# A four-layer network on one core: the scan layer's softplus sum moves to TensorE, and its gate product to GpSimd

## The chip, the core and the metric

The kernel runs on one core of a Trainium2 chip. The time is that of one execution on the device, in microseconds (us); three runs of the kernel before gave a median of 12193.51 us (12187.44 to 12204.01). The core's engines work side by side, each through its own queue in order, and wait for each other through semaphores: TensorE (PE; its weight loads are shown apart, as PEld), VectorE (DVE), ScalarE (ACT), GpSimd (POOL), and SyncE (SP), which here only issues DMA transfers. SBUF is the working memory of 128 partitions, PSUM the small memory that PE writes its results to; in this kernel PE, DVE and ACT work on PSUM, while all of POOL's operands lie in SBUF.

## The reference

Four layers run one after the other on 8 images of 64 channels and 64 x 64 pixels, all in f32. Only the first one is changed, a state-space layer that scans each image in four directions (N = 16 states, DI = 128 inner channels, L = 4096 positions):

```python
xz = einsum('bhwc,dc->bhwd', x, in_proj_w) + in_proj_b
xi, z = split(xz, 2, axis=-1)
xc = silu(dwconv3(transpose(xi), conv_w, conv_b))
...
dts = softplus(einsum('bkrl,kdr->bkdl', dts, dtproj_w) + dtproj_b)
def step(h, inp):
    u_t, dt_t, B_t, C_t = inp
    h = h * exp(dt_t[..., None] * A) + dt_t[..., None] * B_t[:, :, None, :] * u_t[..., None]
    return (h, einsum('bkcn,bkn->bkc', h, C_t))
...
y = ln(y, outnorm_g, outnorm_b, LN_EPS) * silu(z)
return einsum('bhwd,cd->bhwc', y, outproj_w) + outproj_b
```

The two places of the change are the sum inside `softplus`, which the kernel computes as relu(v) + ln(1 + exp(-|v|)), and the product with `silu(z)`, here called the gate. After this layer come an attention layer, an MLP with an inner training loop, and a second attention layer; nothing in them is touched.

## The kernel before

**Chunks and turns.** `scan_layer` goes through 8 images (b = 0 to 7). Each image has 16 chunks: four directions k times four stretches of CH = 1024 positions. Directions 0 and 1 run forward over rows and over columns, 2 and 3 backward; most images take them in the order 0, 2, 1, 3, so that chunk s = 0 to 3 of an image is direction 0, and so on. In a chunk there is one turn for each of the 16 states, n = 0 to 15. One turn works on tiles of 128 channels x 1024 positions:

- `decay` (L762, ACT): a = exp(dt * A), two turns ahead, into one of three buffers, each free again when DVE's scan of three turns before has read it.
- `spread` (L777 or L780), one turn ahead: brings the B row of state n into a PSUM tile `z` of two buffers. In four of the sixteen turns (`BY_POOL`, n = 0, 3, 6, 8) POOL has multiplied it by dt * u already (L770, three turns ahead, on a tile `bt` that DMA fetched), and ACT copies the product to PSUM. In the other twelve PE spreads it by two bf16 matmuls (L780). Buffer z(n) is free when the scan of turn n - 2 is done.
- `unit`: in those twelve turns DVE multiplies z by dt * u (L807); in all of them DVE runs the recurrence along the positions as one scan instruction (L811), and POOL multiplies the result h by the C row `ct` (L816).
- `sum_up` (L882): PE adds the products of all states into the PSUM tile `yps`, two f32 matmuls of 512 columns, LAG = 2 turns behind. In turn 3 it is left out, because `begin_sum` opens the tile of the new chunk there, and in turn 7 (`n == LAG + 5`) it is done twice to catch up.

DVE thus does per turn a scan and in three turns of four a multiply; a PE queue for turn n holds, in this order, `spread(n + 1)`, the sums, one background item, and what the hooks of the turn add.

**Background items.** All other work of the layer (projections of the next image, its layer norm and convolution, and the output of the image before) is cut into items, pairs `(make, use)`, that a `Background` queue hands out one per turn: `make` issues matmuls into a PSUM bank of the pool `psum` (two banks of 512 columns, tag `mm`), `use` takes the bank in the turn after, in `bg.after()`. What is handed to `bg.later` is issued at the start of the next `bg.after()`. In turns 6, 7, 8 (and 9, where the next chunk splits its B rows in three bf16 parts by `rest`, L730 to L736, which happens for directions 0 and 1) no item with matmuls is started. The first items of a chunk are those of `project` for the next chunk: `lower` (L630) and `step_size` (L650), whose result ACT turns into `dt` = relu(v) and `e` = |v| (L658, L659). A convolution (L534, nine taps) is spread over the rest of a chunk's turns in chunks 8 to 15 and holds one of the two banks all the while.

**The two places.** (1) `soft1`, `soft2` and `soft3` are hooked to turns 6, 7 and 8: e = exp(-e) and e = ln(1 + e) on ACT (L664, L667), dt = dt + e on POOL (L670). In turn 11 `step_input` makes dt * u on POOL (L689). The steps of the first four chunks of image 0 (early) and of the last two of image 7 (late) stand at other places. (2) `after`, an image's output, is queued in turn 4 of the next image's first chunk: the norm of y (`norm_y`), and then, for each of 8 blocks of 512 positions, `apply` (a DVE product L475 and an ACT pass L476), `gate` (PE makes z in PSUM, L578; ACT loads the table for Silu, applies it in place, L581, and loads the former table back by `exp_and_ln`, L340; DVE multiplies y by it, L589) and `project_out` (PE, L597 and L598; ACT to `xo`, L604; a DMA out). These items run in chunks 1 to 4 or so of an image, the next image's norm after them, then the convolutions.

Of the kernel before, what the change touches and what calls it, by code (L numbers as in the profile page):

```python
# [3 lines left out]

# [6 lines left out]
F32 = mybir.dt.float32  # L11
BF16 = mybir.dt.bfloat16
AF = mybir.ActivationFunctionType
ALU = mybir.AluOpType
# [230 lines left out]
def scan_layer(cm, x_in, w, xh):  # L245

    tc, nc = cm.tc, cm.nc
    with ExitStack() as ctx:
# [190 lines left out]
        def norm_y(y, blocks, load, gate, project_out):  # L439

            put, chain, sm = inverse_root(len(blocks))
            j0, nb, sq = blocks[0], len(blocks), {}

            def square(j):
                sq[j] = work.tile([128, BK], F32, name="sq", tag="sq")
                nc.scalar.activation(sq[j], y[:, bass.ts(j, BK)], AF.Square)

            def variance(j):
                def make():
                    ps = bank("vps1")  # L450
                    nc.tensor.matmul(
                        ps[:1], lno_avg[:, NBK - 1 : NBK], sq.pop(j), start=True, stop=True
                    )
                    return ps

                def use(ps):
                    put(ps, 1, j - j0)
                    if j + 2 in blocks:
                        square(j + 2)
                    if j - j0 < 3:  # L460
                        load(j)

                return make, use

            def apply(j):
                def make():
                    ps = bank("rps")

                    row = cm.ident[:nb, j - j0 : j - j0 + 1].to_broadcast([nb, DI])
                    nc.tensor.matmul(ps, row, sm["r"], start=True, stop=True)  # L470
                    return ps

                def use(ps):
                    v = y[:, bass.ts(j, BK)]
                    nc.vector.tensor_tensor(v, v, ps, ALU.mult)  # L475
                    nc.scalar.activation(v, v, AF.Identity, bias=on_b, scale=on_g)  # L476

                return make, use

            out = [(None, lambda _: [square(j) for j in blocks[:2]]), none]  # L480
            for j in blocks:
                out.append(variance(j))
            out += chain
            out += [apply(j) for j in blocks[:2]] + [gate(j0)]
            for j in blocks:
                if j + 2 in blocks:
                    out.append(apply(j + 2))
                out += [gate(j + 1) if j + 1 in blocks else none, project_out(j)]
            return out


        FIRST = (range(2), range(2, 3), range(3, 4))
# [71 lines left out]
        def after(b, y, block, blocks=range(NBK)):  # L564

            xf = x_in[b].rearrange("c h w -> c (h w)")
            gated = {}

            def load(j):
                xr = work.tile([C, BK], F32, name="xr", tag="xr", bufs=3)  # L570
                nc.sync.dma_start(xr, xf[:, bass.ts(j, BK)])
                gated[j] = xr

            def gate(j):
                def make():
                    ps = bank("zps")
                    half, x = block(j)
                    nc.tensor.matmul(ps, win[half, 1, :], x, start=True, stop=True)  # L578

                    def silu():  # L580
                        nc.scalar.activation(ps, ps, AF.Silu, bias=inb[:, 1:2])  # L581
                        exp_and_ln()

                    bg.later(silu)
                    return ps

                def use(ps):
                    v = y[:, bass.ts(j, BK)]
                    nc.vector.tensor_tensor(v, ps, v, ALU.mult)  # L589

                return make, use

            def project_out(j):
                def make():
                    po = bank("ops")
                    v = y[:, bass.ts(j, BK)]
                    nc.tensor.matmul(po[:C], cm.ident[:C, :C], gated[j], start=True, stop=False)  # L597
                    nc.tensor.matmul(po[:C], wout, v, start=False, stop=True)  # L598
                    return po

                def use(po):
                    del gated[j]
                    xo = work.tile([128, BK], F32, name="xo", tag="sq")
                    nc.scalar.activation(xo[:C], po[:C], AF.Identity, bias=outb)  # L604
                    bg.later(lambda: nc.sync.dma_start(xh[b][:, bass.ts(j, BK)], xo[:C]))
                    if j + 3 in blocks:
                        load(j + 3)

                return make, use

            return norm_y(y, blocks, load, gate, project_out)
# [8 lines left out]
        def project(u, k, c, low):  # L620

            uo = ordered(u, k, c)
            half = BK // S
            dt = work.tile([DI, CH], F32, name="dt", tag="dt")
            e = work.tile([DI, CH], F32, name="e", tag="e")

            def lower(i):
                def make():
                    ps = bank("dps")
                    nc.tensor.matmul(  # L630
                        ps[: 4 * N].rearrange("p (a b) -> p a b", b=S),
                        wx[:, k, :, :].rearrange("p a m -> p (a m)"),
                        uo[:, i * half : (i + 1) * half, :], start=True, stop=True,
                    )
                    return ps

                def use(ps):

                    nc.scalar.copy(e[: 4 * N, bass.ts(i, BK)], ps[: 4 * N])
                    bg.later(lambda: nc.sync.dma_start(  # L640
                        low["bc"].rearrange("a m l -> (a m) l")[:, bass.ts(i, BK)],
                        e[: 4 * N, bass.ts(i, BK)],
                    ))

                return make, use

            def step_size(i):
                def make():
                    ps = bank("tps2")
                    nc.tensor.matmul(  # L650
                        ps.rearrange("p (a b) -> p a b", b=S), wst[:, k, :],
                        uo[:, i * half : (i + 1) * half, :], start=True, stop=True,
                    )
                    return ps

                def use(ps):
                    b = dtb[:, k : k + 1]
                    nc.scalar.activation(dt[:, bass.ts(i, BK)], ps, AF.Relu, bias=b)  # L658
                    nc.scalar.activation(e[:, bass.ts(i, BK)], ps, AF.Abs, bias=b)  # L659

                return make, use

            def soft1(_=None):
                nc.scalar.activation(e, e, AF.Exp, scale=-1.0)  # L664

            def soft2(_=None):
                nc.scalar.activation(e, e, AF.Ln, bias=1.0)  # L667

            def soft3():
                nc.gpsimd.tensor_tensor(dt, dt, e, ALU.add)  # L670

            ut = {}

            items = [step_size(0), step_size(1)]
            if k < 2:
                low["bc"] = dr.tile([2, 2 * N, CH], F32, name="bc", tag="bc", bufs=8)
                items = [lower(0), lower(1)] + items
            if k % 2:
                ut["u"] = work.tile([DI, CH], F32, name="ut", tag="ut", bufs=1)
                uo = ut["u"].rearrange("p (a b) -> p a b", b=S)  # L680
                nc.scalar.copy(uo, ordered(u, k, c))
                items.insert(0, none)
            else:
                ut["u"] = u[:, bass.ts(c, CH)]
            return dt, ut, e, items, (soft1, soft2, soft3)
# [256 lines left out]
        with tc.manual_schedule():  # L942
# [16 lines left out]
            for b in range(NB):  # L959
                for s in range(4 * NCH):  # L960
# [11 lines left out]
                    if nxt:  # L972
                        do = nxt["pieces"]
                        if early:
                            hooks = {
                                12: [do[0]], 13: [nxt["soft"][2], lambda: step_input(nxt)] + do[1:5],
                                14: do[5:6], 15: do[6:],
                            }
                        else:
                            hooks = dict(zip((5, 7, 8, 9, 10, 13) if parts else (13,), ([f] for f in do)))  # L980
                            for i, f in zip((6, 7, 8), nxt["soft"]):
                                hooks[i] = hooks.get(i, []) + [f]
                            hooks[11] = hooks.get(11, []) + [lambda: step_input(nxt)]

# [6 lines left out]
                    for n in range(N):  # L991
# [6 lines left out]
                        else:  # L998
                            if len(pending) > LAG:
                                sum_up()  # L1000
                            if n == LAG + 5:
                                sum_up()
                            bg.before(n in idle, slots)
                        if (n + 5) % N in BY_POOL and not (early and n + 5 == N):
# [1189 lines left out]
```

## Time and profile before

| | |
|---|---|
| median of three runs | 12193.51 us (12187.44 to 12204.01) |
| profiled execution, own time | 12199.93 us |
| its span, first to last instruction | 12198.2 us |
| mean granted TensorE clock | 0.952 |
| first scan starts / last scan starts | 91.7 / 6916.1 us |
| `ct` products on POOL (L816) | 2048 x 2369 ns |
| `dt + e` on POOL (L670) | 128 x 2364 ns |
| scans on DVE (L811) | 1536 x 2341 ns and 512 x 2281 ns |
| multiplies on DVE (L807) | 1536 x 1211 ns |

Chunks 0 to 15 of image 3 begin at 2684.57, 2734.92, 2786.49, 2841.89, 2899.73, 2957.65, 3010.01, 3062.47, 3116.07, 3166.13, 3219.41, 3270.43, 3321.46, 3371.52, 3423.41 and 3476.83 us (the first scan of each); image 4 follows at 3527.9.

How to read the lines: a timeline line has the start, the duration, the engine, the source line, the operation with the tile written and those read, the shape, and how many instructions in a row it stands for; in brackets, how long the engine had been idle and what ended that. A matmul's duration contains its way through the array, so matmuls that follow each other closely overlap: the distance of two starts is what one costs. The same holds, by less, for DVE and POOL. A line by group has the busy time, the mean duration, and the idle time in front of the group. A line of the waits has the total, the number and the longest.

### The profile page before, as it was taken

To read this page: it belongs to the slowest core of one execution; us is meant where nothing else is said; L and a number is where in the kernel's file an instruction comes from. 1 tells how busy PE (TensorE), PEld (TensorE's weight loads), DVE (VectorE), ACT (ScalarE), POOL (GpSimd) and SP (SyncE) were. 2 spreads that over 40 slices of the span, in tenths; PEclk is the share of its full clock that TensorE was granted. 3 is DMA by queue.
4 is the path that set the end of the run, shared out by engine and by line. 5 is a ranking of instruction groups with operands and counts; after the bars stand their busy time and mean duration, and the time that the engine had idled before them with its cause. 6 is when DMAs were issued, how large, how long until landed. Compare 5 with 4: busy or idle time off the path is not lost. (4 is left out here: it accounts for less than half of the span.)

```text
span 12198.2 us, 120204 instructions
## 1 busy us (share of the span) xinstructions
PE 11171.0 (92%) x39087; PEld 4099.5 (34%) x39087; DVE 10381.2 (85%) x7400; ACT 7575.8 (62%) x10304; POOL 7249.5 (59%) x3326
## 2 busy tenths in 40 slices
PE   7899999999999999999998799999987779999999
PEld 2233333333333333333322233232335463333333
DVE  4999999999999999999999776868677686667767
ACT  4666667767667676676675554646547574555554
POOL 4999999999999999999999600000006490000000
PEclk8999999999999999999999899999998789999999
DMA  3666666666666666666666400000011100000000
GB/s 111 204 212 214 209 209 214 215 211 208 212 212 210 213 214 208 212 215 209 203 203 213 143 24 25 6 24 7 17 42 40 41 22 24 19 4 19 5 11 6
DMA packets 522900, 1528.64 MB, mean 125 GB/s; under 512 B 125312, under 2 KB 142352, under 8 KB 519696
## 3 DMA queue, kind: packets, MB, share of 16 engines
q1 hardware_dynamic: 522256, 1520.80, 37.9%
q8 instruction: 313, 5.13, 0.2%
q14 instruction: 331, 2.71, 0.1%
HBM read 1439.63 MB, written 72.09 MB: 124 GB/s over the span
## 5 line engine op out<-in xcount | busy, mean ns | idle before, releaser
L816 POOL TENSOR_TENSOR ct<-ct,h 128x1024 f32<-128x1024 f32 x2048 | 4796.4, 2369 | 297.0 <-DVE h L811 123.9
L882 PE MATMUL yps<-ct,lno_cen 128*128 128x512 f32 x8192 | 4119.2, 633 | 59.2 <-ACT yps L869 57.8
L811 DVE TENSOR_TENSOR_SCAN h<-a,state,z 128x1024 f32<-128x1024 f32 x1536 | 3571.0, 2341 | 84.0 <-ACT z L777 40.8
L762 ACT ACTIVATE a<-dt,amat 128x1024 f32<-128x1024 f32 x2048 | 2346.9, 1147 | 1136.5 <-DVE h L811 1132.3
L1191 DVE TENSOR_TENSOR sum<-sum,ex 128x1024 f32<-128x1024 f32 x1920 | 2347.9, 1223 | 633.0 <-ACT ex L1184 497.9
L1184 ACT ACTIVATE ex<-sc 128x1024 f32<-128x1024 f32 x2048 | 1968.1, 1024 | 1342.4 <-PE sc L1179 1342.0
L882 PEld LDWEIGHTS yps<-ct,lno_cen 128*128 128x128 f32 x8192 | 1475.9, 195 | 2077.1 <-issue 1810.5
L807 DVE TENSOR_TENSOR z<-z,e 128x1024 f32<-128x1024 f32 x1536 | 1860.0, 1211 | 125.2 <-PE z L780 77.7
L1198 PE MATMUL av<-ex,v 128*64 128x512 f32 x8192 | 1950.0, 604 | 0.0
L1179 PE MATMUL sc<-q,k 16*128 16x512 f32 (+1 forms) x8192 | 1562.2, 623 | 7.3 <-ACT q L1172 6.2
L780 PE MATMUL z<-bs,pick 48*128 48x512 bf16 x3072 | 940.6, 387 | 396.6 <-DVE h L811 348.4
L811 DVE TENSOR_TENSOR_SCAN h<-a,z 128x1024 f32<-128x1024 f32 x512 | 1162.0, 2281 | 81.3 <-ACT z L777 67.3
L770 POOL TENSOR_TENSOR bt<-bt,e 128x1024 f32<-128x1024 f32 x512 | 1212.9, 2369 | 5.2 <-PE cps L392 5.2
L1505 POOL TENSOR_TENSOR gt<-gt,pad 128x1024 f32<-128x1024 f32 x16 | 34.9, 2183 | 1574.3 <-ACT gt L1504 1574.3
L1198 PEld LDWEIGHTS av<-ex,v 128*64 128x64 f32 x8192 | 512.2, 136 | 1332.8 <-issue 1278.9
L1179 PEld LDWEIGHTS sc<-q,k 16*128 16x128 f32 (+1 forms) x8192 | 528.3, 184 | 1021.6 <-issue 976.6
L777 ACT COPY z<-bt 128x1024 f32<-128x1024 f32 x512 | 519.8, 1015 | 402.9 <-DVE h L811 302.9
L780 PEld LDWEIGHTS <-pick 48*128 48x128 bf16 x3072 | 175.4, 95 | 1515.4 <-DVE h L811 930.9
L534 PE MATMUL vps<-pad,convd 128*128 128x512 f32 x1152 | 574.8, 600 | 0.0
L1878 DVE RECIPROCAL r<-e 128x512 f32<-128x512 f32 x128 | 420.7, 3323 | 0.0
L1881 POOL TENSOR_TENSOR r<-r,half 128x512 f32<-128x512 f32 x128 | 162.7, 1271 | 366.7 <-issue 189.4
L798 ACT COPY state<-h 128x1 f32<-128x1 f32 x2048 | 363.1, 177 | 0.0
(417 smaller groups left out, 9581.1 us busy)
## 6 DMA issues: line engine op xcount, KB each, us to landing
ct<-bc SPq DMA_DIRECT2D x2048, 512.0 KB
bt<-bc SPq DMA_DIRECT2D x512, 512.0 KB
x<-x SPq DMA_DIRECT2D x12, 2048.0 KB
bc<-e SPq DMA_DIRECT2D x128, 128.0 KB
x<-x SPq DMA_DIRECT2D x32, 512.0 KB
part<-x SPq DMA_DIRECT2D x128, 128.0 KB
bsd<-bp SPq DMA_DIRECT2D x192, 64.0 KB
bs<-bsd SPq DMA_DIRECT2D x128, 96.0 KB
```

The source lines that it names most:

```text
L534: nc.tensor.matmul(held[0].rearrange("p (r c) -> p r c", c=S), convd[:, t, :], pad[:, j * rows + dy : (j + 1) * rows + dy, dx : dx + S], s ...
L762: ctl["exp", n] = nc.scalar.activation(ctl["a", n], ctl["dt"], AF.Exp, scale=amat[:, ctl["k"], n : n + 1])
L770: nc.gpsimd.tensor_tensor(bt, bt, ctl["dus"], ALU.mult)
L780: nc.tensor.matmul(z[:, bass.ts(i, BK)], pick[:, n : n + 1].to_broadcast([3 * N, DI]), ctl["bs"][:, bass.ts(i, BK)], start=True, stop=True,)
L807: first = nc.vector.tensor_tensor(z, z, ctl["dus"], ALU.mult)
L811: nc.vector.tensor_tensor_scan(h[:, flip], a[:, flip], z[:, flip], 0.0 if state is None else state[:, n : n + 1], ALU.mult, ALU.add,)
L816: freed[at] = nc.gpsimd.tensor_tensor(ct, ct, h, ALU.mult)
L882: nc.tensor.matmul(ctl["ps"][:, bass.ts(i, BK)], lno_cen, ct[:, bass.ts(i, BK)], start=False, stop=(n == N - 1 and not ctl["turns"]),)
L1179: nc.tensor.matmul(sc[:, e, :], k[r : r + d, bass.ts(j, 128)], qs[i][r : r + d, :], start=True, stop=True,)
L1184: nc.scalar.activation(ex, sc, AF.Exp)
L1191: nc.vector.tensor_tensor(sums[i], sums[i], ex, ALU.add)
L1198: nc.tensor.matmul(avs[i][r, :], v[:, j, r], ex[:, e, :], start=(j == 0), stop=(j == TQ - 1))
```

## The change

The softplus sum of a chunk (outside the early and late ones) is made by PE: for each half of 512 columns an identity matmul of `dt` and one of `e` into one PSUM bank, which ACT copies back to `dt` one turn later. The hooks move to turns 5 (exp), 6 (ln), 7 (first half) and 8 (second half), and the second `sum_up` from turn 7 to turn 6. In the gate, ACT's Silu goes from PSUM to a new SBUF tile `zg` one turn later than before (in `use` rather than by `later`), and POOL makes the product with y one turn after that; `project_out(j - 1)` rather than `project_out(j)` is queued behind `gate(j + 1)`. `zg` shares a tag of two buffers with `sq` and `xo`.

```diff
             for j in blocks:
                 if j + 2 in blocks:
                     out.append(apply(j + 2))
-                out += [gate(j + 1) if j + 1 in blocks else none, project_out(j)]
-            return out
+                if j + 1 in blocks:
+                    out.append(gate(j + 1))
+                elif nb < 3:
+                    out.append(none)
+                if j - 1 in blocks:
+                    out.append(project_out(j - 1))
+            return out + [project_out(blocks[-1])]
...
                     nc.tensor.matmul(ps, win[half, 1, :], x, start=True, stop=True)
-
-                    def silu():
-                        nc.scalar.activation(ps, ps, AF.Silu, bias=inb[:, 1:2])
-                        exp_and_ln()
-
-                    bg.later(silu)
                     return ps
 
                 def use(ps):
                     v = y[:, bass.ts(j, BK)]
-                    nc.vector.tensor_tensor(v, ps, v, ALU.mult)
+                    z = work.tile([DI, BK], F32, name="zg", tag="sq")
+                    nc.scalar.activation(z, ps, AF.Silu, bias=inb[:, 1:2])
+                    exp_and_ln()
+                    bg.later(lambda: nc.gpsimd.tensor_tensor(v, v, z, ALU.mult))
...
-            def soft3():
-                nc.gpsimd.tensor_tensor(dt, dt, e, ALU.add)
+            def soft3(i=None):
+
+                if i is None:
+                    nc.gpsimd.tensor_tensor(dt, dt, e, ALU.add)
+                    return
+                ps = bank("sps")
+                at = bass.ts(i, BK)
+                nc.tensor.matmul(ps, cm.ident, dt[:, at], start=True, stop=False)
+                nc.tensor.matmul(ps, cm.ident, e[:, at], start=False, stop=True)
+                bg.later(lambda: nc.scalar.copy(dt[:, at], ps))
...
-                            for i, f in zip((6, 7, 8), nxt["soft"]):
+                            soft = nxt["soft"]
+                            softs = soft if late else (soft[0], soft[1], partial(soft[2], 0), partial(soft[2], 1))
+                            for i, f in zip((6, 7, 8) if late else (5, 6, 7, 8), softs):
                                 hooks[i] = hooks.get(i, []) + [f]
...
-                            if n == LAG + 5:
+                            if n == LAG + 4:
                                 sum_up()
```

More of the change, by code (lines that the diff above doesn't have):

```diff
@@ L3 @@
 from contextlib import ExitStack
+from functools import partial
 import concourse.bass as bass
```

## The prediction

> **What bounds the kernel now.** I read the page's first two parts, then busy time by stretch, then the timelines of VectorE (DVE), GpSimd (POOL) and TensorE (PE) in single chunks, and the waits last. The change touches only the scan layer, the first 57% of the span, where three engines look full:
>
> ```profile
> PE 11171.0 (92%) x39087; PEld 4099.5 (34%) x39087; DVE 10381.2 (85%) x7400; ACT 7575.8 (62%) x10304; POOL 7249.5 (59%) x3326
> ```
> ```profile
> 400.00:6400.00 6000.00, 5647.02 (x13198) 1951.69 (x13196) 5839.45 (x3343) 4156.01 (x6164) 5811.44 (x2506) 0.97 0.64 211
> ...
> 3219.41:3270.43 51.02, 50.30 (x125) 18.14 (x123) 50.59 (x29) 35.95 (x55) 51.02 (x23) 1.00 0.71 222
> ```
>
> The columns are length, then PE, weight loads, DVE, ACT and POOL busy, clock, DMA. The last line is one chunk of sixteen turns (image 3, chunk 10). Which of the three decides is seen from starts, not from busy time:
>
> ```profile
> 3241.39 4.59 DVE L811 TENSOR_TENSOR_SCAN h<-a,state,z 128x1024 f32<-128x1024 f32 x2
> 3245.89 1.21 DVE L807 TENSOR_TENSOR z<-z,e 128x1024 f32<-128x1024 f32 x1
> 3247.14 2.35 DVE L811 TENSOR_TENSOR_SCAN h<-a,state,z 128x1024 f32<-128x1024 f32 x1
> 3249.40 1.21 DVE L807 TENSOR_TENSOR z<-z,e 128x1024 f32<-128x1024 f32 x1
> 3250.64 2.35 DVE L811 TENSOR_TENSOR_SCAN h<-a,state,z 128x1024 f32<-128x1024 f32 x1
> ```
>
> Scan to next start is 2.25 us, multiply to scan 1.24. Sixteen scans and twelve multiplies make 16 x 2.25 + 12 x 1.24 = 50.9 us: the whole chunk (51.02). DVE has no gap, so it is the bound. POOL's products follow each other at 2.32 us (four of L816 in 9.32 us), 22 in a chunk: 51.0. It is level with DVE, but what it makes early (bt) has turns to spare.
>
> PE must hand DVE a new `z` in 12 of 16 turns. Its timeline in turns 6 to 9 of the same chunk:
>
> ```profile
> 3238.54 0.60 PE L780 MATMUL z<-bs,pick 48*128 48x512 bf16 x2
> 3239.07 5.42 PE L882 MATMUL yps<-ct,lno_cen 128*128 128x512 f32 x12
> 3244.42 0.60 PE L780 MATMUL z<-bs,pick 48*128 48x512 bf16 x2
> 3244.95 1.98 PE L882 MATMUL yps<-ct,lno_cen 128*128 128x512 f32 x4
> 3246.77 0.59 PE L730 MATMUL brps<-bw,ident 128*128 128x256 f32 x2
> 3247.20 0.27 PE L732 MATMUL brps<-bp,minus 128*128 128x256 bf16 x1
> 3247.41 0.60 PE L780 MATMUL z<-bs,pick 48*128 48x512 bf16 x2
> ```
>
> No gap here either. An f32 matmul over 512 columns is two records; twelve records from 3239.07 to 3244.42 are 0.43 us each (less a small switch), so 0.86 us per instruction. z(7) starts at 3238.54, z(9) at 3244.42, z(10) at 3247.41. How late may z be? Where DVE does wait for it, the multiply starts 0.81 us after z's first matmul (chunk 13 of the same image):
>
> ```profile
> 3392.15 0.60 PE L780 MATMUL z<-bs,pick 48*128 48x512 bf16 x2
> ...
> 3398.03 0.60 PE L780 MATMUL z<-bs,pick 48*128 48x512 bf16 x2
> ```
> ```profile
> 3392.96 1.23 DVE L807 TENSOR_TENSOR z<-z,e 128x1024 f32<-128x1024 f32 x1 [0.62 <-PE z L780]
> ...
> 3398.84 1.23 DVE L807 TENSOR_TENSOR z<-z,e 128x1024 f32<-128x1024 f32 x1
> ```
>
> So chunk 13 has no slack at z(9); chunk 10 has 3245.89 - 3244.42 - 0.81 = 0.66 us. PE is the hidden second bound, just in these turns.
>
> **The change, part by part.** Counts come from the two programs' instruction orders: POOL -58, DVE -64, ACT +244, PE +488 matmuls, SP none.
>
> **(a) Softplus sum.** 122 of 128 adds `dt + e` leave POOL (2.32 us each, 283 us; the first chunk, three early and two late ones keep theirs). In their place PE gets four identity matmuls (4 x 0.86 = 3.44 us per chunk, 420 us in all) and ACT two copies from PSUM (about 0.58 us each by the 512-column copy L846).
>
> POOL's relief is worth nothing by itself where DVE has no gap: between 0 and the few gaps it causes (DVE's multiply waits 5.0 us on POOL in the stage). I take 0.
>
> The matmuls stand in turns 7 and 8, two in each, in PE's own order: z(7), three sums (the caught-up one moves from turn 7 to 6, still between z(7) and z(9): neutral), sum 0, z(9), one sum, (L730, L732), sum 1, z(10). So z(9) is 1.72 us later and z(10) 3.44. DVE then stalls by the delay less the slack, and after a stall its own clock has moved:
>
> - Chunk 10: z(9) late by 1.72 - 0.66 = 1.06. z(10) starts 3247.41, used 3249.40, slack 1.18: 3.44 - 1.18 - 1.06 = 1.20. Together 2.26.
> - Chunk 13: 1.72 - 0; z(10) starts 3400.48, used 3402.37, slack 1.08: 0.64. Together 2.36.
> - Chunk 5 (no convolution): z(9) 2983.95, used 2985.44, slack 0.68; z(10) 2986.40, used 2988.98, slack 1.77. Together 1.67.
> - Chunk 1: z(9) 2760.19, used 2761.68; z(10) 2763.18, used 2765.21. Together 2.22.
> - Chunk 3 (gates, DVE itself waiting): PE sits idle 1.57 us ahead of z(9), slack 1.29, then 2.34 at z(10). Together 0.
>
> Chunks 8 to 15 are like 10 and 13 (2.3), 0 to 2 like 1 (2.2), 4 to 7 like 5 (1.67), 3 is 0: (8 x 2.3 + 3 x 2.2 + 4 x 1.67) / 16 = 1.98 us, x 122 = **+242 us**. What PE still lags behind turn 10 (1.2 us) it makes up in the gaps of the next chunk's first turns (z(1) of chunk 13 waits 1.80 us for DVE), but where those are short (chunks 0, 8, 9) some stalls come again: between 0 and one more 1.2 us in three chunks of eight images (29), I take +15.
>
> The Trainium skill ("Perfetto Trace Analysis", Identifying the Most-Contended Engine) says matmul busy time tells little of PE's headroom and to judge by the busy share of weight loads. That share is 34%, which would leave room for all 488 matmuls and make this term 0. The twelve starts 0.43 us apart with no gap say otherwise for these turns, and I go by them.
>
> ACT: soft1 and soft2 move to turns 5 and 6, next to step_size's own two ACT passes. An ACT burst there can hold z(8)'s copy: in chunk 10 it has 1.2 us of slack against one pass of 1.05. 0 to +0.2 us per chunk, and a stall there would be taken out of the one at z(9): 0. Where a convolution holds one of the two PSUM banks and `brps` needs one too (chunks 8, 9, 10, 15), sum 1 waits for the cast of brps, 0.37 us and a handover, about 0.5: 0 to 32 x 0.5 = 16, I take +8.
>
> **(b) Gate.** 64 multiplies leave DVE:
>
> ```profile
> L589 DVE TENSOR_TENSOR y<-zps,y 128x512 f32<-128x512 f32 x48 | 32.2, 670 | 6.8 <-ACT zps L581 6.4
> ```
>
> Start to next start it is 0.58 us (2004.47 to 2005.05): 64 x 0.58 = **-37 us**, all on DVE's path. POOL gets 64 of about 1.27 us (128x512 products L1881), 81 us, less than the 283 it lost. The rule against it is in the Trainium skill ("GPSIMD Engine Reference", Engine selection): elementwise work belongs on VectorE, twice as fast. By the two durations alone that would cost 64 x 0.60 = +38; but DVE is the engine without a gap.
>
> Silu now runs one turn after its matmul rather than in the same turn, so ACT no longer stands waiting for PE:
>
> ```profile
> ACT zps L581 <- PE zps L578: 44.4, 30, 4.8
> ACT L581 <- PE zps L578: 42.6, 13, 6.8
> ```
>
> DVE's longest gaps of the stage (2.42 us before the scan of turn 6 in image 3, chunk 3, ended by ACT's copy of z) come from such bursts. That gap recurs in chunks 3 and 4 of an image, 8 x 2 x 2.2 = 35 at most. Table loads and Silu itself stay, ACT gains copies: 0 to -35, I take -15.
>
> New waits: Silu writes a buffer of two (shared with xo), so it waits for POOL's product of an earlier gate, and the last project_out waits for POOL where it waited for DVE. Behind Silu stand ACT's decays, which have two turns to spare. 0 to 8 x 1.5 = 12, I take +4. At the layer's end two gates lie in a bare chain: 2 x 0.6 = +1.
>
> Sum: 242 + 15 + 8 - 37 - 15 + 4 + 1 = **+218 us** on the profiled execution, 12199.9 (span 12198.2). The median of the three times, 12193.5, is 6.4 lower, so 12193.5 + 218 = **12412 us**, 1.8% slower.
>
> **Rivals.**
>
> 1. *Faster.* PE is not the bound in turns 7 to 9: the stall per chunk stays under 0.43 us, where 122 of them equal the gains of 37 + 15. For it: chunk 3 absorbs everything, and PE has over 2 us of gaps per chunk elsewhere. Against it: the four other chunks I read have 0 to 0.68 us of slack at z(9) against 1.72. With no stall the time is 12193 - 37 - 15 = 12141; if POOL's relief and ACT's also close half of the 165 us that DVE idles before its scans and multiplies (65.5 + 68.1 + 32.0 from 400 to 6900): 12193 - 52 - (83 - 15) = 12073.
> 2. *Slower by far less.* z(9) is absorbed and only z(10) stalls: between z(9) and z(10) PE needs a sum (1.82), sum 1 (1.72) and z (0.53) = 4.07, where DVE needs 3.5. That is 0.57 per chunk: 122 x 0.57 - 52 = +18, 12211.
> 3. *Slower by far more.* All 3.44 us add to every chunk (no slack counts, PE becomes the bound throughout): 420 - 37 = 12577.
> 4. *POOL's gate product becomes the wait.* If ACT waits for POOL one product (2.3 us) at each gate: 64 x 2.3 = +147 on top, 12559. For it: POOL at 5811 of 6000 us. Against: it loses 283.
>
> **How the numbers follow.** Forecast 0.74 (12290 to 12510); rival 1 0.09; rival 2 0.08; rivals 3 and 4 0.09. The low end cuts rival 1 and part of rival 2, the high end reaches half way to rivals 3 and 4: 12260 to 12530. About 0.2% (24 us) is what a measurement here tells from no change: rival 2 straddles it, half same, half slower. Faster 0.09, same 0.04, slower 0.87.
>
> **What the profile after would show.** Right: the DVE multiplies of turns 9 and 10 idle for 1 to 2 us each before them, ended by PE's z, in most chunks from 5 on; PE without gaps from turn 5 to 15; POOL's share down by 200 us and idle more; no DVE gate lines; chunks 8 to 15 near 53 us rather than 51. Wrong: those gaps absent and chunks still 51 us; or gaps ended by ACT's z copy (then the copies are to blame), or by POOL. What would make it wrong most: a turn-6 start of PE earlier than 1.3 us after DVE's scan of turn 5, as sums moved forward fall into gaps I counted as full.

## The result and the profile after

The changed kernel takes 12418.03 us (median of 4 runs, 12416.46 to 12424.47), the kernel before 12192.65 in the same series: a ratio of 1.0182 with a 95% interval of 1.0166 to 1.0198, 1.8% slower. The forecast was 12412 us.

The loss lies in the scan layer to the last microsecond: the last scan starts at 7135.2 us instead of 6916.1, 219.1 later, and the span is 218.5 longer. The first line is the page's busy time of the changed kernel; the second, its busy time in the same stretch as shown of before (length, PE, weight loads, DVE, ACT, POOL, clock, DMA).

```profile
PE 11506.0 (93%) x40063; PEld 4259.5 (34%) x40063; DVE 10364.8 (83%) x7336; ACT 7714.7 (62%) x10548; POOL 7061.7 (57%) x3268
```
```profile
400.00:6400.00 6000.00, 5765.36 (x13705) 2037.43 (x13704) 5649.84 (x3185) 4141.53 (x6194) 5454.93 (x2368) 0.99 0.62 204
```

In these 6000 us DVE is busy 5650 instead of 5839 and POOL 5455 instead of 5811: both stand idle more than before. Chunk 13 of image 3 shows why; this is PE's timeline, turns 6 to 9:

```profile
3487.87 0.60 PE L791 MATMUL z<-bs,pick 48*128 48x512 bf16 x2
3488.40 5.42 PE L893 MATMUL yps<-ct,lno_cen 128*128 128x512 f32 x12
3493.65 1.02 PE L679 MATMUL sps<-dt,ident 128*128 128x512 f32 x2
3494.51 1.02 PE L680 MATMUL sps<-e,ident 128*128 128x512 f32 x2
3495.47 0.60 PE L791 MATMUL z<-bs,pick 48*128 48x512 bf16 x2
3496.00 1.98 PE L893 MATMUL yps<-ct,lno_cen 128*128 128x512 f32 x4
3497.82 1.02 PE L679 MATMUL sps<-dt,ident 128*128 128x512 f32 x2
3498.68 1.02 PE L680 MATMUL sps<-e,ident 128*128 128x512 f32 x2
3499.63 0.60 PE L791 MATMUL z<-bs,pick 48*128 48x512 bf16 x2
```

From z(7) to z(9) PE needs 3495.47 - 3487.87 = 7.60 us; before the change it was 5.88. DVE's timeline of the same turns has the wait:

```profile
3489.94 4.59 DVE L822 TENSOR_TENSOR_SCAN h<-a,state,z 128x1024 f32<-128x1024 f32 x2
3496.28 1.23 DVE L818 TENSOR_TENSOR z<-z,e 128x1024 f32<-128x1024 f32 x1 [1.75 <-ACT dt L681]
3497.54 2.35 DVE L822 TENSOR_TENSOR_SCAN h<-a,state,z 128x1024 f32<-128x1024 f32 x1
3500.37 1.23 DVE L818 TENSOR_TENSOR z<-z,e 128x1024 f32<-128x1024 f32 x1 [0.48 <-ACT dt L681]
```

The prediction had 1.72 and 0.64 for this chunk. The multiply starts 0.81 us after z(9)'s first matmul, as it did before wherever DVE waited for PE. But the trace names something else as what ended the wait: ACT's copy of the sum to `dt`.

```profile
3495.57 0.59 ACT L681 COPY dt<-sps 128x512 f32<-128x512 f32 x1 [2.02 <-PE sps L680]
```

From 400 to 6900 us that name has the largest total of DVE's waits, which is why it needed an experiment:

```profile
DVE z L818 <- ACT dt L681: 190.4, 189, 2.2
...
DVE z L818 <- PE z L791: 49.9, 81, 2.2
```

All gaps of DVE over 0.06 us between the first and the last scan, added up from the trace, are 204 us before and 439 after; those ahead of turns 9 and 10 alone (of their multiply or scan) 38 and 239. The 235 us more of gaps, 22 us because an instruction behind a gap no longer starts before the one ahead of it has ended (in the lines of before, a scan of 2.35 us is followed after 2.25), and 37 us less of work on DVE make up the 219 us, to 1 us.

### The profile page after: what moved, and what is told of

It reads as the page before. It is cut to its first block, busy times and chain, and to the rows that moved or that the text cites. A ratio compares the mean times of both kernels' runs of the same rounds, so it can differ in the third digit from the quotient of the medians.

```text
span 12416.7 us, 122384 instructions
## 1 busy us (share of the span) xinstructions
PE 11506.0 (93%) x40063; PEld 4259.5 (34%) x40063; DVE 10364.8 (83%) x7336; ACT 7714.7 (62%) x10548; POOL 7061.7 (57%) x3268
## 5 line engine op out<-in xcount | busy, mean ns | idle before, releaser
L893 PE MATMUL yps<-ct,lno_cen 128*128 128x512 f32 x8192 | 4065.3, 626 | 59.0 <-ACT yps L880 58.8
```

The costliest lines, as they stand in the source:

```text
L893: nc.tensor.matmul(ctl["ps"][:, bass.ts(i, BK)], lno_cen, ct[:, bass.ts(i, BK)], start=False, stop=(n == N - 1 and not ctl["turns"]),)
```

## The experiments

**Each part alone.** *Gate only:* the kernel before with the new gate.

```diff
-                    bg.later(silu)
...
-                    nc.vector.tensor_tensor(v, ps, v, ALU.mult)
+                    z = work.tile([DI, BK], F32, name="zg", tag="sq")
+                    nc.scalar.activation(z, ps, AF.Silu, bias=inb[:, 1:2])
+                    exp_and_ln()
+                    bg.later(lambda: nc.gpsimd.tensor_tensor(v, v, z, ALU.mult))
```

> The kernel before with part (b) alone (gate product on GpSimd, Silu a turn later). Theory A (the loss is all in the identity matmuls of turns 7 and 8; the gate is a gain): 64 x 0.58 = 37 us of VectorE work go, and the gap before the scan of turn 6 in gate chunks (5.4 us per image in the kernel before, 0 in the changed one) goes too, 43 at most: 12193 - 37 - (15 to 43) = 12113 to 12141 us. Theory B (the gate product, queued on a GpSimd engine that is as full as VectorE, costs part of the loss): no gain or slower than 12193, since GpSimd's adds of the softplus sum are back here.

Measured: 12178.9 us against 12187.7, ratio 0.9994 (0.9984 to 1.0003). Not told from no change: the gain of theory A is not there. Theory B's "no gain" came true, but that a full POOL is the reason isn't shown by it (*room on GpSimd*, below, tests that). *Sum only:* the changed kernel with the gate of before.

```diff
-                    z = work.tile([DI, BK], F32, name="zg", tag="sq")
...
+                    nc.vector.tensor_tensor(v, ps, v, ALU.mult)
```

> The changed kernel with the gate as before: part (a) alone. Theory A: the changed kernel without the gate's gain, 12418 + 37 + (15 to 43) = 12470 to 12498 us, if the two parts add up. Theory B: below 12418.

Measured: 12454.9, ratio 1.0218 (1.0201 to 1.0235): not below 12418 as theory B had it, but 15 us short of theory A's range too, which took the two parts to add up. So the sum costs 267 us, and where it is in place the gate gives back 37 (12455 to 12418, which come from different series; 42 if each is taken against the kernel before of its own series); alone it gives 9. The two ratios of the 37 carry intervals of 0.0016 and 0.0017 to each side, some 28 us for the difference, so that the gate gave more beside the sum than alone is likely rather than shown.

**PE or ACT.** *Matmuls alone:* four identity matmuls in turns 7 and 8 of the kernel before, on constant data, read by nothing.

```diff
+            def load_pe():
+                ps = bank("sps")
+                m = convd[:, 0:4, :].rearrange("p a b -> p (a b)")
+                nc.tensor.matmul(ps, cm.ident, m, start=True, stop=False)
+                nc.tensor.matmul(ps, cm.ident, m, start=False, stop=True)
...
+                            if not late:
+                                for i in (7, 8):
+                                    hooks[i] = hooks.get(i, []) + [nxt["extra"]]
```

> The kernel before, GpSimd's add and hooks kept, with the four identity matmuls added in turns 7 and 8 on constant data into a bank that nothing reads (their result is not used). No ACT copies, no moved soft steps, gate as before. Theory A: the same stalls of z in turns 9 and 10, 242 + 15 + 8 = 265 us: about 12458 (12400 to 12500). Theory C: 12193, no change.

Measured: 12453.9, ratio 1.0218 (1.0201 to 1.0235): as expected by theory A, and the same as the whole of part (a), with some 29 us of uncertainty on the difference. With no copy there to be named, the trace now names PE. The first line is from the kernel before, the second from this run:

```profile
DVE z L807 <- PE z L780: 41.3, 46, 2.9
```
```profile
DVE z L815 <- PE z L788: 252.7, 264, 2.2
```

*Copies alone:* the other half (the edit is shown against *matmuls alone*).

```diff
-                nc.tensor.matmul(ps, cm.ident, m, start=True, stop=False)
-                nc.tensor.matmul(ps, cm.ident, m, start=False, stop=True)
+                bg.later(lambda: nc.scalar.copy(ps, convd[:, 0:4, :].rearrange("p a b -> p (a b)")))
```

> The kernel before with only the two ACT copies of 512 columns added, in turns 8 and 9, from a constant in SBUF into a PSUM bank that nothing reads (their result is not used). Theory A (TensorE alone): no loss, 12188 to 12200 us. Theory C (ACT's copies): up to the 230 us of the change.

Measured: 12182.0 against 12187.2, ratio 0.9997 (0.9988 to 1.0006). ACT's copies cost nothing (at most 7 us by the interval); theory C falls. These copies don't wait for PE as those of the changed kernel do (2.02 us in the line above); that the real ones cost nothing either follows, within the 29 us, from *sum only* being no slower than *matmuls alone*. In the changed kernel the copy of one half and z(9) both follow the same identity matmul: in chunk 13 the copy ended at 3496.16 (it starts at 3495.57 and takes 0.59), 0.12 us before DVE's multiply, so it was merely the later of two events.

*One product:* half the matmuls.

```diff
-                nc.tensor.matmul(ps, cm.ident, dt[:, at], start=True, stop=False)
-                nc.tensor.matmul(ps, cm.ident, e[:, at], start=False, stop=True)
+                nc.tensor.matmul(ps, cm.ident, e[:, at], start=True, stop=True)
```

> The changed kernel with one identity matmul per half instead of two (the matmul of e alone; the relu part of the sum is left out, so dt is not the softplus). TensorE gets 0.86 us more in turn 7 and in turn 8 rather than 1.72; ACT's two copies stay as they are. Theory A (TensorE late with z): redoing my five chunks with half the delay gives 0.20 + 0.34 in chunk 10, 0.86 + 0 in chunk 13, 0.18 in chunk 5, 0.50 in chunk 1, 0 in chunk 3; weighted (8 x 0.7 + 3 x 0.5 + 4 x 0.18) / 16 = 0.49 us x 122 = 60, so about 12193 + 60 + 8 - 37 - 35 = 12190, 12170 to 12240. Theory C (ACT's copies of dt, which the trace names as what ends VectorE's gaps, hold it up): the time stays near 12418.

Measured: 12274.9, ratio 1.0070 (1.0053 to 1.0087): far from 12418, so theory C falls here too, but outside 12170 to 12240. The direction is A's, and so are the turns. In image 3 the gaps ahead of turns 9 and 10 are 0.89 and 0.16 in chunk 1 (I had 0.18 and 0.32), 0.68 and 0 in chunk 5 (0.18 and 0), 0.17 and 0.89 in chunk 10 (0.20 and 0.34), 0.89 and 0 in chunk 13 (0.86 and 0); chunk 3 has 1.20 (0), as with the gate only. Over the layer they are 93 us, 55 more than before, where I had 60. The miss lies elsewhere: the expectation took 72 us off for the gate. In the trace DVE has 38 us less work, but its gaps ahead of turn 8 alone are 67 us instead of 19 (40 with the gate only, 32 with *soft steps early*, below). All gaps together are 107 us more than before and 13 us of overlap are lost, which with the 38 makes up, to 1 us, the 81 by which the last scan is further from the first.

**The smaller terms.** *Catch-up back:* the changed kernel with the second sum in turn 7 again.

```diff
-                            if n == LAG + 4:
+                            if n == LAG + 5:
```

> The changed kernel with the second sum of a chunk back in turn 7. My reading calls its place neutral, since it stands between z(7) and z(9) in both: 12408 to 12428 us. If the move was what loads turn 6 to 9, the time falls well below 12400.

Measured: 12417.5 (12407.1 to 12425.8) against 12418.0 of the changed kernel, neutral as read. *Soft steps early:* the kernel before with exp and ln moved.

```diff
-                            for i, f in zip((6, 7, 8), nxt["soft"]):
+                            for i, f in zip((6, 7, 8) if late else (5, 6, 8), nxt["soft"]):
```

> The kernel before with exp and ln of the softplus in turns 5 and 6 (GpSimd's add stays in turn 8): the price of the ACT burst alone. My reading: 0 to 0.2 us per chunk, 12188 to 12212 us.

Measured: 12204.1 against 12187.2, ratio 1.0011 (1.0002 to 1.0021): some 13 to 17 us, within what was expected; the price of the ACT burst. Ahead of turn 8, whose z ACT copies, DVE's gaps grow from 18 to 32 us.

**Why the gate gives so little alone.** In gate only, chunks 2 and 3 of an image are shorter as forecast (means over images 1 to 6, from the starts of their scans: 55.5 to 53.9 and 57.6 to 55.2 us), but chunk 4 is longer, 55.7 to 57.6, and so is image 7, where outputs come in pairs of blocks, 859.5 to 866.9. From the first to the last scan DVE has 40 us less work in the trace, but 15 us more of gaps and 7 us less of overlap. In chunk 4 there is one gap of 4.9 us per image. These are ACT's, POOL's and DVE's timelines around it in image 3:

```profile
2909.26 0.18 ACT L800 COPY state<-h 128x1 f32<-128x1 f32 x1
2916.04 0.68 ACT L606 ACTIVATE xo<-ops,outb 64x512 f32<-64x512 f32 x1 [6.60 <-POOL y L591]
2916.63 1.04 ACT L666 ACTIVATE e<-e 128x1024 f32<-128x1024 f32 x1
2917.57 1.00 ACT L779 COPY z<-bt 128x1024 f32<-128x1024 f32 x1
```
```profile
2910.12 2.36 POOL L772 TENSOR_TENSOR bt<-bt,e 128x1024 f32<-128x1024 f32 x1
2912.45 2.34 POOL L818 TENSOR_TENSOR ct<-ct,h 128x1024 f32<-128x1024 f32 x1
2914.76 1.25 POOL L591 TENSOR_TENSOR y<-y,zg 128x512 f32<-128x512 f32 x1
```
```profile
2918.68 2.29 DVE L813 TENSOR_TENSOR_SCAN h<-a,z 128x1024 f32<-128x1024 f32 x1 [4.94 <-ACT z L779]
```

`xo` and `zg` share two buffers. At the end of an image's output three `project_out` follow the last `gate`, the second of their `xo` needs the buffer of the last `zg`, and that is free when POOL has made its product, which stands behind a bt and a ct product. ACT waits 6.60 us in order, and z's copy and DVE's scan behind it. *Gate spaced* puts two empty items there (the edit is shown against *gate only*):

```diff
+            if nb > 2:
+                out[-1:-1] = [none, none]
             return out + [project_out(blocks[-1])]
```

> The gate part alone, with two empty items between project_out(5) and project_out(6). The gate part alone measured 12179, where ACT waits 44.3 us in 7 places for GpSimd's last gate product of an image, whose buffer xo needs. Theory D (that wait ate the gate's gain): the wait goes, and 20 to 40 us of VectorE's gaps in chunk 4 with it: 12140 to 12160 us. Rival: the gain is lost to GpSimd being full (gate products and the softplus adds together); then 12175 to 12185.

Measured: 12192.1 against 12187.2, ratio 1.0001 (0.9992 to 1.0010): above the rival's range as well. The wait for `xo` is gone and the gaps of chunk 4 fall from 6.7 to 2.2 us per image, but chunk 5 has 5.6 instead of 0.5. Nor is the wait for POOL's product gone altogether: it has moved to the last Silu of an image's output, which needs one of the same two buffers, in five images:

```profile
ACT zg L591 <- POOL y L593: 18.8, 5, 3.8
```

So theory D got no clean test: the stall is real, but moving the items makes others. What the new gaps in chunk 5 are (they stand ahead of several turns, some with POOL waiting for a `ct` transfer) wasn't settled.

*Room on GpSimd*, the other explanation: the adds left out, with the gate moved and not moved.

```diff
-                nc.gpsimd.tensor_tensor(dt, dt, e, ALU.add)
+                pass
```

> The gate part alone, with GpSimd's add of the softplus sum left out (dt is then relu(v) alone): 122 + 6 adds of 2.32 us less on GpSimd, no identity matmuls on TensorE. Theory E (the gate's gain needs the room on GpSimd that part (a) makes; without it the gate product takes the place of the DVE work as the wait): 12187 - 37 = 12150 or below, down to 12110 if the turn-6 gaps stay away. Theory F (what ate the gain is the order of the output items, and GpSimd's room is nothing): as the gate alone, 12175 to 12195.

> The kernel before with GpSimd's add of the softplus sum left out (dt is relu(v) alone), gate as before: the worth of GpSimd's relief by itself, which I put at 0. Theory E: with the gate on VectorE, VectorE stays the bound: 12170 to 12190. If GpSimd is a second bound beside VectorE: below 12160.

Measured in one series, before 12194.2: with the gate moved 12170.5, ratio 0.9981 (0.9972 to 0.9990); not moved 12176.5, ratio 0.9985 (0.9976 to 0.9994). The relief by itself is worth some 18 us (7 to 29), and the gate's gain beside it is 6, with some 15 to each side. Theory E falls: room on POOL does not bring the 37 us. Theory F's range is missed too, by 5 us.

**Without the sum.** The sum can be left away altogether: ln(1 + exp(v)) needs no relu part, at the price that exp(v) must stay finite.

```diff
-                    nc.scalar.activation(dt[:, bass.ts(i, BK)], ps, AF.Relu, bias=b)
-                    nc.scalar.activation(e[:, bass.ts(i, BK)], ps, AF.Abs, bias=b)
+                    nc.scalar.activation(dt[:, bass.ts(i, BK)], ps, AF.Exp, bias=b)
...
-                nc.scalar.activation(e, e, AF.Exp, scale=-1.0)
+                pass
...
-                nc.scalar.activation(e, e, AF.Ln, bias=1.0)
+                nc.scalar.activation(dt, dt, AF.Ln, bias=1.0)
...
-                nc.gpsimd.tensor_tensor(dt, dt, e, ALU.add)
+                pass
```

> A version without the sum: dt = ln(1 + exp(v)) by two ACT functions, in place of relu(v) + ln(1 + exp(-|v|)) (right as long as exp(v) stays finite in f32, v below 88), and the gate part. No add on GpSimd, no identity matmuls, and per chunk ACT has 2 x 0.68 + 1.05 us less. Theory E: as the gate without the add or better by the gaps that ACT bursts make: 12090 to 12150, faster than both kernels.

> The same direct softplus with the gate as before. Theory E: VectorE keeps its 37 us of gate products: 12130 to 12190, about 37 above the version with the gate moved.

Measured: with the gate moved 12156.5, ratio 0.9965 (0.9951 to 0.9979); with the gate as before 12131.1, ratio 0.9949 (0.9935 to 0.9962). Both are faster than both kernels. But the version with the gate moved missed its range by 7 us, and the order of the two is the reverse of what was expected: the gate move now costs 25 us (with some 24 to each side). The version with the gate on DVE is 45 us faster than the one that only leaves out the add. Ahead of turns 6 to 8 its DVE gaps are 39 us, there 77, and 82 in the kernel before; turn 6 is where ACT's pass of exp(-e) stood, which falls away, and ACT is busy 3972 us of the 6000 instead of 4167. That its fewer passes are the cause is likely, not shown. In all, DVE's gaps are 140 us instead of 204, and it is busier than in any other kernel here:

```profile
400.00:6400.00 6000.00, 5659.96 (x13326) 1955.68 (x13325) 5895.17 (x3379) 3972.46 (x5883) 5621.12 (x2418) 0.98 0.64 213
```

## Why the prediction was right

**The bound.** PE as the hidden second bound in turns 7 to 10: shown, since matmuls that nothing reads lengthened the layer by the whole amount of part (a). DVE as the first bound fits its few gaps before (204 us in 6824), but taking work off it isn't worth what the work takes: 9 us of 37 with the gate only.

**Part (a), sum of 242 + 15 + 8 = 265.** The sum alone cost 267, the matmuls alone 266. By class of chunk the working held as well. With the matmuls alone, gaps ahead of turns 9 and 10 are 1.93 us per chunk (mean over images 1 to 6; I had 1.98): 2.17 in chunks 8 to 15 (2.3), 2.18 in 0 to 2 (2.2), 1.74 in 4 to 7 (1.67), 0 in 3 (0). Single chunks of image 3 fit less well: 1.75 + 0.48 in chunk 13 (1.72 + 0.64), but 1.55 + 1.75 in chunk 10 (1.06 + 1.20), 1.75 + 1.02 in chunk 1 (1.04 + 1.18), 1.75 + 0.48 in chunk 5 (1.04 + 0.63). In those three the slack that I had read at z(9) is gone, or nearly so. In chunks 1 and 10 PE comes to z(7) later than in the kernel before, by 1.37 and 0.58 us counted from the chunk's first scan. In chunk 5 what I read as slack (0.68) was mostly DVE's own waiting: 0.28 and 0.32 us for POOL, which are not there with the matmuls. The stalls that I took to come again in the next chunk's first turns (+15) are there in size but not in place: gaps grow by 14 us ahead of turns 11 to 13 and by 4 ahead of turns 0 to 5.

The bank that `brps` and the sum share does cost what I put at half a microsecond, here 0.46, on PE in chunk 10 of the changed kernel; with the matmuls alone it is 8.8 us in 19 places (I took 8):

```profile
3338.95 0.27 PE L743 MATMUL brps<-bp,minus 128*128 128x256 bf16 x1
3339.68 1.12 PE L679 MATMUL sps<-dt,ident 128*128 128x512 f32 x2 [0.46 <-ACT bp L747]
```

and so DVE's second stall there is 1.75 rather than the 1.20 worked out without it:

```profile
3336.97 1.23 DVE L818 TENSOR_TENSOR z<-z,e 128x1024 f32<-128x1024 f32 x1 [1.03 <-ACT dt L681]
3338.24 2.35 DVE L822 TENSOR_TENSOR_SCAN h<-a,state,z 128x1024 f32<-128x1024 f32 x1
3342.34 1.23 DVE L818 TENSOR_TENSOR z<-z,e 128x1024 f32<-128x1024 f32 x1 [1.75 <-ACT dt L681]
```

ACT's moved passes were put at 0 of a bound of 0.2 us per chunk (24 us); alone they cost 13 to 17. That a stall of theirs would be taken out of the one at z(9) is seen in the sums: ahead of turn 8 DVE's gaps are 37 us with the sum only and 8 with the matmuls alone, ahead of turns 9 and 10 they are 241 and 265. POOL's relief was put at 0, with 5 us as the most that it could be, and is about 18 by itself. The two are small and of opposite sign, so that part (a) came within 2 us of its sum is partly luck.

The Trainium skill ("Perfetto Trace Analysis", Identifying the Most-Contended Engine) has PE's headroom judged by the busy share of weight loads, beside the share of peak FLOPs, which wasn't worked out here. The first of the two does not show the headroom in these turns: it is 34% over the kernel before and after, and 36% in chunk 10 before (18.14 of 51.02 us), and yet the 488 matmuls cost 0.55 us of the kernel's time each.

**Part (b), -37 - 15 + 4 + 1 = -47.** Beside the sum the gate gave -37; here two terms were mis-sized, in opposite directions. The gaps ahead of turn 6 that ACT's wait for PE made went nearly whole (43 us to 7, where I took 15 of 35). The new wait for POOL's product, bounded at 12, was larger: in the changed kernel ACT waits 28.6 us for it in 7 places, with a gap of 3.9 us on DVE ahead of turn 8 in chunk 4 of images 1 to 6 (23 us), and image 7 takes 10.4 us longer than with the sum only. Together -37 - 36 + 23 + 10 = -40. What I missed is the buffer: I costed the wait of Silu for an earlier product, not that of an `xo` for the last `zg`. I also called the 2.42 us ahead of turn 6 DVE's longest gap; the waits list has one of 2.9 us for PE's z and one of 3.0 for Silu.

**The sum of all** came to +218 on the profiled execution, and the measured profiled executions are 12199.9 and 12418.5. That it agrees to 1 us is partly luck, as the terms above show.

**The rivals.** Rival 1 needed a stall under 0.43 us per chunk; ahead of turns 9 and 10 it was 1.7 in the changed kernel and 1.9 with the matmuls alone. Rival 2 wanted z(9) absorbed: with the matmuls alone it is so in chunk 3 only. In the changed kernel it is so in chunk 4, where DVE has just waited 3.9 us ahead of turn 8, and nearly so in chunk 8. Rival 3 fails by 160 us: slack does count. Rival 4's mechanism is there once per image, not 64 times.

**The signs to look for.** Right were POOL's longer idle times (its ct products wait 465 us for DVE instead of 67), POOL's busy time down by 188 us, and chunks 8 to 15 at 52.4 to 55.2 us. The gaps in turns 9 and 10 are there, but a whole microsecond or more in fewer chunks than I had written: from chunk 5 on, 42 of 88 ahead of turn 9 and 32 ahead of turn 10. PE is without a gap from turn 5 to 15 in three of the chunks 8 to 15 of image 3 and has one of up to 1 us in each of the other five. Wrong was the name at the gaps' end: I had written PE's z, and that a copy of ACT as releaser would put the blame there; it was another copy of ACT, that of the sum, and the experiments say it isn't to blame.

## What to carry to other kernels

An engine can be second in the sum of its busy time and yet be the first to run late in a few turns of a loop: before work is moved to it, look at those turns, at the distance from its hand-over to the use, with the buffers that limit how far it may run ahead. A releaser named in a trace need only be the event that came last, not the one that was missing (here 190 us were put down to a copy that costs nothing); put each suspect into the kernel alone, as a load that nothing reads, to tell them apart. And before a sum is moved from engine to engine, ask whether it is needed: here the form without it was the only one that still computes all of the layer and is faster beyond its interval.

## What was not expected

Matmuls on constant data that nothing reads cost 266 us, as much as the real ones with their copies and waits (267, with some 29 us on the difference): the cost is their place in PE's queue, with the bank they share, and not what becomes of the sum. The change of the gate, one and the same edit, is worth -37 us beside the sum, -9 alone, -6 without the add and +25 with the direct softplus: with some 12 to 28 us of uncertainty on each, the ends of that row are apart, its middle isn't. What it depends on, the crowding of ACT's and POOL's turns perhaps, no run here settles. TensorE's mean granted clock was higher in the slower kernel, 0.958 against 0.952, but also in the fastest one here, the direct softplus with the gate as before (0.954 to 0.956).
